# A graph kernel that fetches one edge tile in 22 row by row, and stores its results later

## The chip, the cores and the metric

The kernel runs on one core of one Trainium2 chip. The metric is the time of one execution on the device in microseconds (us). A core has several engines with instruction queues of their own, each working in order: TensorE (PE, matrix products; PEld is its loading of weights), VectorE (DVE), ScalarE (ACT), GpSimd (POOL) and SyncE (SP). SP, ACT and POOL also issue DMAs. Where a line of a profile says SPq or ACTq, it is an instruction that the engine's queue issues itself, such as a DMA.

## The reference

The input is a graph with 12,500 nodes of 256 features and 212,500 edges, sorted by destination. Each edge has a source, a destination and one of 8 types.

```python
h = jnp.maximum(_layernorm(x, axis=-1), 0.0)
hx = jnp.einsum('ni,rio->rno', h, weight)          # 8 weights of 256 x 256
msg = hx[edge_type, src]
agg = jax.ops.segment_sum(msg, dst, num_segments=12500)
out = x + agg * 0.5**0.5 + h_bias + (h @ loop_weight) * 0.5**0.5
```

## The kernel before

**Order of the sums.** The kernel does not compute 8 products per node and then gather them. It first adds up, for each destination and each type, the normalized rows `h` of the sources, and multiplies these sums by the weights afterwards. The edges stand in 1581 tiles of 128 places, two tiles to a unit. For each tile the 128 rows of `h` that its edges name are brought into a buffer `msg` (128 rows of 256 float32). PE multiplies them by a one-hot matrix of destination and type (`edge_sums`, line 1005, four matmuls a tile), so that a unit's sums per destination and type stand in PSUM (`ps`). DVE adds them to a ring of sums in SBUF (`acc`, line 1031). When all edges of a group of 128 nodes are through, PE multiplies the group's sums by the weights (`group_work`, line 1187, 36 matmuls a group), DVE adds `x` and the bias (lines 1200 and 1201), and once four groups are ready SP stores them with one DMA of 512 KB (line 1206). There are 98 groups; the last two are stored on their own (line 1203).

**Phases.** In the first 140 us or so the rows of `x` are normalized and written to `h32` in DRAM. The first 100 tiles gather rows of `x` itself and normalize them in place on ACT. All later tiles fetch from `h32`.

**Two ways to fetch a tile.** The usual one is an indirect DMA on POOL's queue (`gather`, line 915), one instruction for the 128 rows. The other is used for one tile in SINGLE = 28, those with `t % 28 == 27`, once `h32` has been complete for long enough and not for the last 16 tiles. Its 128 rows are fetched by 128 DMAs of 1 KB, 64 on SP's queue and 64 on ACT's (`load_sources`, line 939). Before each 32 rows the queue loads their addresses into registers with one TENSOR_LOAD (line 931). PE counts the 128 arrivals on one of four semaphores before it sums the tile.

**The written order.** The order of all instructions is written out by hand (`tc.manual_schedule`). A loop runs over the tiles; in step `t` it emits the sums of tile `t`, the gathers for tiles further ahead (64 ahead at first, 24 from about tile 370 on, down to 8 at the end: `goal`), and parts of the other work. A gather also waits for the latest unit summed at that point of the order. For a row-fetched tile the step FAR = 36 tiles ahead takes the buffer (`begin_fetch`); HOLD = 8 steps later its instructions begin to be emitted, FETCH = 4 per step on each queue:

```python
if t + FAR >= gathered and single_rows(t + FAR):
    begin_fetch(t + FAR)
while gathered < min(NT, goal(t)):
    gather(gathered)
    gathered += 1
fetch(FETCH)
```

The message buffers are a pool of 33 pairs of tiles (MSGS = 66), taken in turn. The rows of `x`, of `h` for the nodes' own part, and the results share a pool of six buffers of 512 KB (`rowp`). The result is added into the buffer that held the group's `x`, and the store reads it from there.

**What else is in these queues.** SP also loads `x` and `h` for the next four groups (line 1137) and, once per block of 128 units, the indices of a later block (line 393). ACT loads that block's `spans` (line 405, eight small DMAs), and clears parts of the ring early on (line 1040). From 300 us on ACT computes nothing. An instruction that waits holds up all that follow in its queue: in SP's, a store that waits for its sums stands in front of the row fetches emitted after it.

## Time and profile before

| | |
|---|---|
| median of 3 runs | 1983.34 us (1980.15 to 1984.99) |
| the profiled execution | 1982.09 us; span 1980.4 us |
| mean granted TensorE clock | 0.949 |
| busy: PE, DVE, POOL, ACT | 1711.7, 1309.2, 1457.9, 159.2 us |
| indirect DMAs on POOL | 1431 from `h32`, 100 from `x` |
| row DMAs | 3200 on SP, 3200 on ACT |
| DMA over the span | 279.45 MB, mean 141 GB/s |

In the lines of the profile a group of instructions stands as line, engine, operation, result <- operands, count, followed by busy time, mean duration and the idle time in front of it with what ended it. In the views of one line, three numbers with strokes are the shortest, the median and the longest duration in ns, followed by the first and the last start in us. A wait line reads: who waited, for whom, total us, times, longest. A line of the timeline reads: start, duration, what, and in brackets the idle time before it.

### The profile page before, as it was taken

Reading aid. Unit: us, or ns where it says so; the run is one execution under the profiler, and the core shown is the slowest. Engines: PE = TensorE matmul, PEld = TensorE weight load, DVE = VectorE, ACT = ScalarE, POOL = GpSimd, SP = SyncE. Lnnn points to the kernel's source line nnn. Section 1 sums busy time; section 2 is a strip of 40 time slices with the busy share of each in tenths; the row PEclk is TensorE's granted clock in tenths of the full one; section 3 lists DMA queues with packets and bytes.
Section 4 is the critical chain, followed back from the end, with each engine's and each line's share of the span. In section 5 each row is a group of like instructions: output and inputs, shape, how many; then the busy total and the mean of one; then the engine's idle time right before and its main releaser. Section 6 shows DMA issues by size and latency. Waiting matters only on the chain. (4 is left out here: it accounts for less than half of the span.)

```text
span 1980.4 us, 41340 instructions
## 1 busy us (share of the span) xinstructions
PE 1711.7 (86%) x10161; PEld 1473.8 (74%) x10161; DVE 1309.2 (66%) x3272; ACT 159.2 (8%) x334; POOL 1457.9 (74%) x1557
## 2 busy tenths in 40 slices
PE   2348999998899888889998898888989989899998
PEld 1247898997777777778777777777777767687897
DVE  6769767886665677656678565578666567665653
ACT  6777200000000000000000000000000000000000
POOL 7677776677777777777777777777777777777774
PEclk8559999999999999999999999999999999999999
DMA  7993444443444444444434444444444344444432
GB/s 252 358 301 103 126 126 134 140 140 107 138 128 122 149 132 120 141 130 121 149 111 141 132 119 143 141 119 141 129 122 142 109 144 130 120 140 125 127 115 78
DMA packets 158363, 279.45 MB, mean 141 GB/s; under 512 B 35376, under 2 KB 109126, under 8 KB 158118
## 3 DMA queue, kind: packets, MB, share of 16 engines
q0 software_dynamic: 73488, 200.77, 34.5%
q1 hardware_dynamic: 76584, 72.73, 11.9%
q10 hardware_dynamic: 8046, 3.30, 0.9%
q8 instruction: 80, 1.31, 0.3%
q14 instruction: 165, 1.35, 0.2%
HBM read 251.06 MB, written 25.60 MB: 140 GB/s over the span
## 5 line engine op out<-in xcount | busy, mean ns | idle before, releaser
L915 POOL DMA_INDIRECT msg<-h,gidx x1431 | 1361.2, 951 | 458.6 <-issue 335.6
L1005 PEld LDWEIGHTS ps<-oh,msg 128*128 128x128 f32 x6324 | 942.1, 198 | 408.1 <-DMA msg<-h,gidx 258.7
L1005 PE MATMUL ps<-oh,msg 128*128 128x136 f32 (+2 forms) x6324 | 1022.8, 291 | 226.3 <-DMA msg<-h,gidx 139.0
L1187 PE MATMUL po<-w,acc 128*128 128x256 f32 x3136 | 891.0, 389 | 15.4 <-DVE acc L1031 15.3
L1031 DVE TENSOR_TENSOR acc<-acc,ps 128x352 f32 x791 | 408.8, 517 | 413.0 <-PE ps L1005 402.1
L1187 PEld LDWEIGHTS po<-w,acc 128*128 128x128 f32 x3136 | 519.0, 193 | 52.1 <-DVE acc L1031 18.6
L1069 DVE SCALAR_TENSOR_TENSOR acc<-types,pt 128x256 f32<-128x256 bf16 (+1 forms) x688 | 247.3, 411 | 67.6 <-PE pt L1051 61.9
L967 DVE TENSOR_TENSOR oh<-fixed,cols 128x544 f32<-128x544 f32 (+1 forms) x396 | 285.8, 722 | 0.0
L915 POOL DMA_INDIRECT msg<-in_x_dram,gidx x100 | 94.8, 948 | 41.4 <-issue 30.1
L1187 PE MATMUL po<-wl,self_t 128*128 128x256 f32 x392 | 115.5, 420 | 3.5 <-DVE acc L1031 1.8
L1187 PEld LDWEIGHTS po<-wl,self_t 128*128 128x128 f32 x392 | 73.8, 210 | 12.6 <-DVE acc L1031 3.1
L853 ACT ACTIVATE msg<-msg,shift,rstd 128x256 f32<-128x256 f32 x100 | 50.8, 586 | 4.4 <-DVE stats L817 3.6
L853 ACT ACTIVATE xt<-xt,shift,rstd 128x256 f32<-128x256 f32 x98 | 50.0, 587 | 7.0 <-DVE shift L850 6.1
L809 DVE BATCH_NORM_STATS2 stats<-xt 128x6 f32<-128x256 f32 x98 | 34.3, 412 | 23.5 <-DMA xt<-in_x_dram 22.7
L1200 DVE TENSOR_TENSOR xr<-xr,po 128x256 f32<-128x256 f32 x98 | 40.4, 412 | 13.4 <-PE po L1187 12.2
L1123 DVE CAST types<-pt 128x512 bf16<-128x512 f32 x22 | 15.2, 691 | 49.6 <-PE pt L1119 49.6
L1056 DVE COPY self_t<-pt 128x256 f32<-128x256 f32 x98 | 40.7, 415 | 8.5 <-PE pt L1051 5.4
L1051 PE MATMUL pt<-ident,hr 128*128 128x128 f32 x196 | 38.9, 281 | 7.2 <-DMA hr<-h 5.3
L442 DVE TENSOR_SCALAR moves<-fixed 128x271 int32<-128x271 int32 (+1 forms) x90 | 40.6, 452 | 4.4 <-DVE acc L1031 3.0
L1201 DVE TENSOR_TENSOR xr<-xr,po 128x256 f32<-128x256 f32 x98 | 41.2, 421 | 3.4
L444 DVE COPY_PREDICATED fixed<-moves,fixed 128x311 int32<-128x311 int32 (+14 forms) x90 | 38.0, 422 | 3.1
L1051 PEld LDWEIGHTS pt<-ident,hr 128*128 128x128 f32 x196 | 25.6, 153 | 10.6 <-DMA hr<-h 5.6
(162 smaller groups left out, 349.1 us busy)
## 6 DMA issues: line engine op xcount, KB each, us to landing
msg<-h ACTq DMA_DIRECT2D x3200, 1.0 KB
msg<-h SPq DMA_DIRECT2D x3200, 1.0 KB
msg<-h,gidx POOLq DMA_INDIRECT x1431
xt<-in_x_dram SPq DMA_DIRECT2D x24, 512.0 KB
h<-xt SPq DMA_DIRECT2D x24, 512.0 KB
xr<-in_x_dram SPq DMA_DIRECT2D x24, 512.0 KB
hr<-h SPq DMA_DIRECT2D x24, 512.0 KB
out_dram<-xr SPq DMA_DIRECT2D x24, 512.0 KB
```

The costliest lines, as they stand in the source:

```text
L442: nc.vector.tensor_single_scalar(m, packed[:, :n], 1 << (bit + k), op=ALU.bitwise_and)
L853: nc.scalar.activation(row, row, AF.Relu, bias=shift[:n, j : j + 1], scale=rstd[:n, j : j + 1])
L915: i = nc.gpsimd.indirect_dma_start(out=msg[t], out_offset=None, in_=table[:, :], in_offset=bass.IndirectOffsetOnAxis(ap=gidx[b][:, at : at ...
L967: j = nc.vector.tensor_tensor(o[:, k : k + v, :i, :width], iota_f[:, :width].unsqueeze(1).unsqueeze(1).to_broadcast([P, v, i, width]), of. ...
L1005: j = nc.tensor.matmul(ps[:, c, first : first + width], m[:, c * P : (c + 1) * P], o[:, :width], start=(i == 0 and c == 0), stop=(end and ...
L1031: i = nc.vector.tensor_tensor(a, a, ps, op=ALU.add)
L1051: in_run("turns", nc.tensor.transpose(pst[:, c, :n], rows_[:n, c * P : (c + 1) * P], ident[:n, :n]), c == KC - 1)
L1056: nc.vector.tensor_copy(got["self", g][:, :, :n], pst[:, :, :n])
L1069: i = nc.vector.scalar_tensor_tensor(acc[:, :, r, s0 : s0 + n], of, float(r + 1), pst[:, :, :n], op0=ALU.is_equal, op1=ALU.mult)
L1187: i = nc.tensor.matmul(got["out", g][:n], lhs, rhs, start=(r == R and c == 0), stop=(r == R - 1 and c == KC - 1))
L1200: nc.vector.tensor_add(rows_[:n, k, :], rows_[:n, k, :], outs[g % 2][:n, 1, :])
L1201: nc.vector.tensor_add(rows_[:n, k, :], rows_[:n, k, :], got["out", g][:n])
```

## The change

Three constants and the place of the stores change. SINGLE goes from 28 to 22, so that one tile in 22 is fetched row by row. FAR goes from 36 to 44, so that such a tile's buffer is taken 44 tiles ahead of its sums. The store of four groups' results is no longer emitted when they are finished but STORE = 24 steps later; whatever is left is emitted after the loop. HOLD, FETCH and the pools stay. Everything behind the changed lines moves by one line (939 becomes 940), and by a few more towards the end.

```diff
-SINGLE = 28
+SINGLE = 22
 FETCH = 4
 SOURCES = 32
 BY_SP = (0, 2)
 HOLD = 8
-FAR = 36
+FAR = 44
+STORE = 24
...
                 elif k == XG - 1:
                     first = plan.starts[XG * q]
-                    nc.sync.dma_start(
-                        out[first : d0 + n].rearrange("(k p) d -> p k d", p=P), rows_)
+                    stores.append((done["tile"] + STORE, lambda: nc.sync.dma_start(
+                        out[first : d0 + n].rearrange("(k p) d -> p k d", p=P), rows_)))
...
                     gather(gathered)
                     gathered += 1
+                while stores and stores[0][0] <= t:
+                    stores.pop(0)[1]()
                 fetch(FETCH)
...
             while held():
                 advance(None)
+            while stores:
+                stores.pop(0)[1]()
             state["general"] = nc.values_load(flag[0:1, 0:1], min_val=0, max_val=1)
```

## The prediction

> **What bounds the kernel now.** First the page: span, busy shares and the costliest group.

> ```profile
> span 1980.4 us, 41340 instructions
> PE 1711.7 (86%) x10161; PEld 1473.8 (74%) x10161; DVE 1309.2 (66%) x3272; ACT 159.2 (8%) x334; POOL 1457.9 (74%) x1557
> L915 POOL DMA_INDIRECT msg<-h,gidx x1431 | 1361.2, 951 | 458.6 <-issue 335.6
> L915 POOL DMA_INDIRECT msg<-in_x_dram,gidx x100 | 94.8, 948 | 41.4 <-issue 30.1
> ```

> PE has the largest share (86%), POOL only 74%, but POOL's idle time belongs to "issue", a wait for nothing. So next the timeline of POOL in the middle, POOL's gathers of line 915 between 600 and 1950 us, and three stretches of the windows (columns PE, PEld, DVE, ACT, POOL).

> ```profile
> 1001.74 0.95 POOL L915 DMA_INDIRECT msg<-h,gidx  x1 [0.30 <-DMA msg<-h,gidx]
> 1002.99 0.95 POOL L915 DMA_INDIRECT msg<-h,gidx  x1 [0.30 <-issue]
> 1004.24 0.94 POOL L915 DMA_INDIRECT msg<-h,gidx  x1 [0.30 <-issue]
> ...
> L915 POOL DMA_INDIRECT msg<-h,gidx x1073: 942/946/1279, 600.2 to 1948.9; - x179
> ...
> 250.00:300.00 50.00, 50.00 (x334) 46.25 (x333) 31.32 (x66) 3.82 (x2) 35.69 (x39) 1.00 0.44 125
> 1000.00:1050.00 50.00, 43.79 (x253) 37.30 (x252) 35.11 (x79) 0.00 (x0) 37.79 (x41) 0.93 0.44 130
> 1850.00:1900.00 50.00, 49.80 (x295) 45.76 (x296) 29.63 (x62) 0.00 (x0) 37.80 (x40) 1.00 0.40 119
> ```

> A gather starts every 1.25 us, whatever the releaser column names: 0.95 busy and 0.30 between. From 600 to 1949 us there are 1072 such steps in 1348.7 us, 1.258 each. PE is full only early (250 to 300) and late (1850 to 1900); at 1000 us it has 6 us free in 50. The waits agree: PE waits for gathered messages, and SP for the sums in front of its stores.

> ```profile
> PE ps L1005 <- DMA msg<-h,gidx: 139.0, 218, 3.4
> PEld ps L1005 <- DMA msg<-h,gidx: 258.7, 372, 3.8
> SPq L1206 <- DVE acc L1031: 245.6, 16, 24.0
> SPq L1206 <- DVE xr L1201: 186.3, 5, 87.7
> ```

> No line there names a row-fetched tile: those arrive in time. So POOL, with 1531 gathers at 1.25 to 1.26 us, sets the pace.

> **Fewer gathers.** The row fetches are counted in the list of DMA issues and placed by line 939's rows.

> ```profile
> msg<-h ACTq DMA_DIRECT2D x3200, 1.0 KB
> msg<-h SPq DMA_DIRECT2D x3200, 1.0 KB
> ...
> L939 ACTq DMA_DIRECT2D msg<-h x3200: 217/228/835, 229.7 to 1843.9; - x189
> L939 SPq DMA_DIRECT2D msg<-h x3200: 227/228/1229, 232.4 to 1905.7; - x189
> ```

> Each of the two queues issues 64 rows per fetched tile: 50 tiles, t = 167, 195, ..., 1539. The same conditions with 22 in place of 28 give t = 175, 197, ..., 1561, which is 64 tiles. POOL loses 14 gathers: 14 x 1.258 = 17.6 us. If nothing else came late, the profiled 1982.1 us would become 1964.5.

> **More rows.** The two queues gain 14 x 64 = 896 rows each, and have 22 tiles of time, not 28, for one fetched tile. In the old rhythm 27 gathers give 27 x 1.258 = 34.0 us; in the new one 21 give 26.4 us. What a fetched tile costs its queue is read where a queue runs without a gap: from one TENSOR_LOAD (line 931, addresses of 32 rows) to the next is half a tile.

> ```profile
> L931 ACTq TENSOR_LOAD <-single x9: 2239/2280/2332, 227.0 to 331.4; - x9
> ...
> L931 ACTq TENSOR_LOAD <-single x11: 2248/2279/2355, 403.3 to 535.8; - x11
> ...
> L931 ACTq TENSOR_LOAD <-single x11: 2249/2307/2513, 1590.9 to 1722.3; - x11
> ...
> L931 SPq TENSOR_LOAD <-single x4: 2057/2158/2212, 427.9 to 466.7; - x4
> ...
> 920.57 5.01 ACTq L405 DMA_DIRECT2D spans<-in_dst_dram  x8
> ...
> L405 ACTq DMA_DIRECT2D spans<-in_dst_dram x35: 317/434/1652, 359.0 to 1590.5; - x35
> ...
> L1206 SPq DMA_DIRECT2D out_dram<-xr x24: 384/415/426, 227.9 to 1950.9; - x24
> L1137 SPq DMA_DIRECT2D xr<-in_x_dram x25: 371/405/2164, 129.3 to 1906.0; - x25
> L1137 SPq DMA_DIRECT2D hr<-h x25: 459/512/2182, 130.0 to 1819.5; - x25
> ```

> ACT: 104.4 us for 8 halves, 132.5 for 10, 131.4 for 10; together 368.3 / 28 = 13.15, so **26.3 us a tile** (26.1 to 26.5 by stretch). SP: 38.8 us for 3 halves, one load of x among them: 12.8 to 12.9, or 25.7 a tile; the 24 stores and some 45 loads of x and h at 0.4 to 0.5 us, spread over 64 tiles, add 0.5: 26.2 to 26.3. ACT adds its 35 loads of spans at up to 5.01 / 8 = 0.63: about 20 us in all. POOL needs 26.4 us for the same 22 tiles. The three are level, and that is the heart of this prediction: the row queues have had a quarter of their time free, and after the change they have none.

> ACT's sum, the slower of the two: its first TENSOR_LOAD at 227.0 stays, since the clear that stands in front of it waits for PE (row below); 128 halves x 13.15 = 1683; spans 20; the last row is issued at about 1930. Its landing shows nowhere by itself: the nearest row is a gather's landing, 2.79 us, in the chain that ended last; I bound it by 1 and 3 and take 2.5. Tile 1561 can be summed at 1933.

> ```profile
> 227.04 1.91 ACT L1040 ACTIVATE acc<-zero 128x2048 f32<-128x2048 f32 x1 [16.06 <-PE po L1187]
> ...
> 1955.17 2.79 DMA msg<-h,gidx
> ...
> L1005 PE MATMUL ps<-oh,msg x80: 312/313/417, 1936.7 to 1967.5; 128*128 128x176 f32 x80
> ...
> 1955.36 2.23 PE L1005 MATMUL ps<-oh,msg 128*128 128x176 f32 x12 [1.38 <-DMA msg<-h,gidx]
> 1958.00 0.86 PE L1005 MATMUL ps<-oh,msg 128*128 128x176 f32 x4 [0.41 <-DMA msg<-h,gidx]
> ```

> A tile has four matmuls of line 1005, so the last 80 are tiles 1561 to 1580, and 1561 starts at 1936.7 now. From there to 1982.1 are 45.4 us; some 2 of them are waits for gathers that would have landed. 1933 + 43.4 = 1976.4 for an execution like the profiled one. With gathers alone tile 1561 would start at 1919. The rows, 14 us late by then, give back 12 of the 17.6 us.

> **Lead of 44 tiles and later stores.** The longer lead holds a buffer 8 tiles longer. Of 66 tiles' buffers, 24 tiles of gathers ahead plus two or three fetched pairs are in use; I cost it at nothing, bounded by 0 and one gather step per fetched tile if a gather had to wait for a buffer. The stores' 432 us of waiting on SP (245.6 + 186.3) disappear from in front of the rows: SP will reach a store after its data is ready. That saves no time by itself, because PE never waited for a fetched tile; it is what lets SP take the extra rows at all. What stands behind a store in SP's queue (rows, loads of x and h, the indices of a later block) is pulled earlier by it. The result buffer is held 24 tiles longer of some 65 tiles per four groups, and its next user is two rounds off: nothing. The last stores stay where they are, at the end of the program. What is new: SP and ACT, without slack, run just in time, so that loads of x, h and indices come some 20 tiles after their place in the program. The first use of x or h is 30 tiles or more after it, that of the indices about 20: a wait of 0 to 4 us on DVE, five times, which DVE (66% busy) mostly hides.

> [...]

> **Rivals.**

> *The rows hide (chance 0.25).* A fetched tile at or below 26.1 us, as in ACT's first stretch, less waiting between POOL's and ACT's delays: the whole 17.6 us are gained, 1964.5. For it: the bound is missed by only 1 or 2%. Against it: the other two stretches.

> *The row queues are slower when they never rest (0.20; slower than before).* Each 0.1 us on a fetched tile costs 63 x 0.1 = 6.3 us at the end, and from 26.5 us on the time passes 1989. The rows of line 931 over the whole run show where this would come from:

> ```profile
> L931 ACTq TENSOR_LOAD <-single x100: 2216/2300/3672, 227.0 to 1831.0; - x100
> L931 SPq TENSOR_LOAD <-single x100: 2044/2180/3600, 228.9 to 1893.3; - x100
> ```

> If one TENSOR_LOAD in eight took the longest 3.67 us, a tile would cost 0.34 more: 1976 + 21 = 1997. Against it: in 227 to 331 us both queues were full, and ACT's halves were the shortest of all.

> *Both queues take turns at a shared generator (0.02).* Rows of 0.228 us would queue behind the other's 0.228: 64 x 0.456 + 5.6 = 34.8 us a tile, 540 us more. Against it: the stretch from 227 to 331 with both busy and no such lengthening. [...]

> *PE takes over (0.03).* It is full in 1850 to 1900, so the gain of the gathers after 1850 (1 of the 14) could go: 1966.

> **How the numbers follow.** The likeliest case (0.50) is the row queues as the new bound, 1970 to 1988, at 1976.4; the profiled execution (1982.1) lies 1.2 under the median of the runs (1983.3), so 1977 for the median. About 0.3%, 6 us, is what can be told from no change: below 1977.4 is faster, above 1989.3 slower. Faster: hidden rows 0.25, PE 0.03 and somewhat under half of the likeliest case, 0.20: 0.48. Slower: 0.22 by the two slow cases. The rest, 0.30, is within. The range runs from 1963 (hidden rows, with 1 us of spread) to 1996 (one long load in eight).

> **What would show it.** Right: 4096 rows per queue, 1517 gathers; SP's wait for stores near nothing; TENSOR_LOADs of ACT at a steady 13.1 to 13.2 us to the end, the last rows at 1920 to 1940; PE waiting before fetched tiles from about t = 500 on, and POOL ahead by more tiles. Wrong: ACT's last row well before 1915 (the rows hide), halves of 13.3 us or more (slower), or POOL's gathers waiting for buffers.

## The result, and the profile after

The kernel after takes **2155.1 us** (median of 4 runs, 2151.1 to 2158.5) against 1984.1 for the kernel before (a fourth run has joined the three of the table above): ratio 1.086, 95% interval 1.083 to 1.089. The forecast was 1977, and its range ended at 1996. The profiled execution has a span of 2149.4 us. When the first eight runs of the experiments were made, the kernel before itself took 2398 to 2401 us instead of 1980 to 1984, with pauses of some 0.7 us between and in instructions of SP and ACT, so those eight are compared only with each other, and the later ones with 1980 to 1984.

The page of after, and its queues:

```profile
span 2149.4 us, 45059 instructions
PE 1776.7 (83%) x10161; PEld 1514.3 (70%) x10161; DVE 1313.6 (61%) x3272; ACT 159.2 (7%) x334; POOL 1441.4 (67%) x1543
q1 hardware_dynamic: 78376, 73.65, 11.3%
q10 hardware_dynamic: 9838, 4.22, 1.2%
L916 POOL DMA_INDIRECT msg<-h,gidx x1417 | 1344.7, 949 | 644.1 <-issue 303.5
```

The counts came out as forecast: 14 gathers fewer (1417 and 100), and POOL busy for 16.5 us less. But POOL's idle time in front of the gathers rose from 458.6 to 644.1 us. The same stretches of the windows show the pace:

```profile
250.00:300.00 50.00, 50.00 (x334) 46.24 (x334) 31.23 (x66) 1.91 (x1) 35.50 (x38) 1.00 0.48 136
1000.00:1050.00 50.00, 39.45 (x219) 30.95 (x218) 21.71 (x47) 0.00 (x0) 32.26 (x35) 0.97 0.42 116
1850.00:1900.00 50.00, 42.38 (x248) 33.58 (x246) 26.07 (x59) 0.00 (x0) 33.77 (x37) 1.00 0.40 110
```

At 1000 us PE does 219 matmuls where it did 253, and POOL 35 gathers where it did 41. Every engine does less in the same time, so somebody waits for a transfer. The waits say for which:

```profile
PE ps L1006 <- DMA msg<-h,gidx: 211.0, 263, 3.2
PEld ps L1006 <- DMA msg<-h,gidx: 352.3, 415, 3.6
PE ps L1006 <- PEq L1003: 30.5, 9, 5.8
POOL msg L916 <- DMA msg<-h,gidx: 223.3, 291, 3.0
SPq L1207 <- DVE xr L1202: 51.1, 2, 50.8
SPq L1207 <- DVE acc L1032: 20.8, 8, 5.7
```

`msg<-h,gidx` is a gather. PE waits for **gathers** 211 us (139 before), for fetched tiles (the wait of line 1003) only 30 us, nine times. POOL itself waits 223 us for earlier gathers to land (54.9 before). In these sums each wait holds the 0.30 us that stand in front of every gather (303 ns at the least, in all 1530 steps of before and all 1516 of after); without them, 291 waits are 136 us in after, 145 are 11 us before.

Of the 169 us by which the span grew, 72 are PE's longer waits for gathers, 30 its waits for fetched tiles, and 65 are PE's own busy time: the same 10161 matmuls took 1776.7 us instead of 1711.7, at a mean granted clock of 0.921 instead of 0.949. A slower PE does not explain the loss, since PE waits longer for its gathers as well.

The row queues hardly rest either (SP waits for 71 us in all between 600 and 1800 us). In that time 82 steps of ACT from one TENSOR_LOAD to the next, half of its share of a tile, are 14.55 us on the mean, and 81 of SP's 14.62:

```profile
L932 ACTq TENSOR_LOAD <-single x83: 2223/2296/3352, 604.6 to 1797.8; - x83
L932 SPq TENSOR_LOAD <-single x82: 2114/2184/3498, 603.1 to 1787.4; - x82
```

A stretch of POOL's timeline:

```profile
953.51 0.94 POOL L916 DMA_INDIRECT msg<-h,gidx  x1 [0.30 <-issue]
955.29 0.94 POOL L916 DMA_INDIRECT msg<-h,gidx  x1 [0.83 <-PE ps L1006]
957.94 0.95 POOL L916 DMA_INDIRECT msg<-h,gidx  x1 [1.71 <-DMA msg<-h,gidx]
960.27 0.94 POOL L916 DMA_INDIRECT msg<-h,gidx  x1 [1.38 <-DMA msg<-h,gidx]
```

Before, a gather started every 1.25 us whatever the releaser column said. Here it starts after 1.78, 2.65 and 2.33 us: POOL has up to eight gathers in flight and then starts the next when the oldest has landed (when a gather of after starts, at most seven others are under way, in 563 of 1517 cases just seven, and none starts sooner than 0.257 us after the eighth before it has landed; 0.259 us in before, 0.26 in the run micro below). The chip has fewer gathers to do and is later with each.

**Why they land late** is in the trace's DMA packets. The trace gives a packet's queue but not its engine. These are the packets of after that follow each other without a gap in one stretch; others of POOL's queue, which overlap them, are left out (start in ns by the trace's own clock, 10,468 ns ahead of the views', queue, duration in ns, bytes; 1 is SP's queue, 10 ACT's, 0 POOL's; a 4-byte packet of 1 or 10 that follows a row is the write that counts it as done: with 896 rows more on queue 10, after has 896 packets of 1 KB and 896 of 4 bytes more there than before):

```
956570  10   46  1024
956613  10    9     4
956619  10   54  1024
956665  10   14     4
956673  10  102  1024
956769  10   12     4
956775  10  205  1024
956974  10   12     4
956980   1  180  1024
957154   1   12     4
957160  10  180  1024
957334  10   12     4
957340   1   47  1024
957383   1    9     4
957389   0  493  4096
957879   1  181  1024
```

Each packet begins within 10 ns of the end of the one ahead of it, whichever queue it is from: **all rows go through one DMA engine**, where a gather also has its share, by an even division two packets of 4 KB (a gather is 32 of those, and 16 counts of 4 bytes: 48,544 and 24,272 for the 1517 gathers of after; the page has 16 engines). Between 700 and 1500 us 1066 rows of ACT's queue lie clear of SP's loads and stores; 12 of them overlap another row by more than 10 ns. Of the gathers' packets that fit into the chain of rows, 23% take over 0.6 us; of those that overlap a row, and so are on another engine, 0.06% do, and 98 of 100 take 0.16 to 0.42 us. I call a gather's packet of over 0.6 us a slow one and count them per gather from 600 to 1600 us: **0.23 before, 0.56 after**. A gather has landed when the last of its 16 counts has come: of the gathers that start from 600 to 1600 us and show all 16, 569 in after, the 15th count comes 2.8 us after the start (median) and the 16th 10.3 us; in before 2.8 and 4.4 us. In after one count of sixteen is late, as one engine of sixteen would make it.

The rows wait there as well. Taking ACT's n-th row packet for its n-th issue, from 600 to 1800 us a row's packet ends 7.0 us after its issue in after (median) and 1.5 us before. A line of rows stands in front of that engine.

### The profile page after: what moved, and what is told of

Same layout as the page of the kernel before. It is cut to its first block, busy times and chain, and to the rows that moved or that the text cites. A ratio compares the mean times of both kernels' runs of the same rounds, so it can differ in the third digit from the quotient of the medians.

```text
span 2149.4 us, 45059 instructions
## 1 busy us (share of the span) xinstructions
PE 1776.7 (83%) x10161; PEld 1514.3 (70%) x10161; DVE 1313.6 (61%) x3272; ACT 159.2 (7%) x334; POOL 1441.4 (67%) x1543
## 5 line engine op out<-in xcount | busy, mean ns | idle before, releaser
L916 POOL DMA_INDIRECT msg<-h,gidx x1417 | 1344.7, 949 | 644.1 <-issue 303.5
L1006 PEld LDWEIGHTS ps<-oh,msg 128*128 128x128 f32 x6324 | 966.0, 203 | 538.4 <-DMA msg<-h,gidx 352.3
L1006 PE MATMUL ps<-oh,msg 128*128 128x136 f32 (+2 forms) x6324 | 1056.6, 298 | 333.1 <-DMA msg<-h,gidx 211.0
L1188 PE MATMUL po<-w,acc 128*128 128x256 f32 x3136 | 908.3, 395 | 13.0 <-DVE acc L1032 13.0
L1188 PEld LDWEIGHTS po<-w,acc 128*128 128x128 f32 x3136 | 531.2, 198 | 49.4 <-DVE acc L1032 14.3
L1188 PE MATMUL po<-wl,self_t 128*128 128x256 f32 x392 | 124.2, 446 | 3.4 <-DVE acc L1032 1.8
L916 POOL DMA_INDIRECT msg<-in_x_dram,gidx x100 | 94.8, 948 | 41.5 <-issue 28.0
L1188 PEld LDWEIGHTS po<-wl,self_t 128*128 128x128 f32 x392 | 79.1, 224 | 13.5 <-DVE acc L1032 2.6
L1201 DVE TENSOR_TENSOR xr<-xr,po 128x256 f32<-128x256 f32 x98 | 40.5, 413 | 15.4 <-PE po L1188 14.2
L1052 PEld LDWEIGHTS pt<-ident,hr 128*128 128x128 f32 x196 | 26.5, 157 | 10.3 <-DMA hr<-h 5.3
```

The lines of the kernel that those rows point to most:

```text
L916: i = nc.gpsimd.indirect_dma_start(out=msg[t], out_offset=None, in_=table[:, :], in_offset=bass.IndirectOffsetOnAxis(ap=gidx[b][:, at : at ...
L1006: j = nc.tensor.matmul(ps[:, c, first : first + width], m[:, c * P : (c + 1) * P], o[:, :width], start=(i == 0 and c == 0), stop=(end and ...
L1052: in_run("turns", nc.tensor.transpose(pst[:, c, :n], rows_[:n, c * P : (c + 1) * P], ident[:n, :n]), c == KC - 1)
L1188: i = nc.tensor.matmul(got["out", g][:n], lhs, rhs, start=(r == R and c == 0), stop=(r == R - 1 and c == KC - 1))
L1201: nc.vector.tensor_add(rows_[:n, k, :], rows_[:n, k, :], outs[g % 2][:n, 1, :])
```

## Experiments

The theory before the runs: that engine is full, 0.8 us per gathered tile plus 0.1 us per row (worked out from the paces of before and after, 1.213 and 1.345 us per tile). The rivals: the row queues' issuing; the buffers taken 44 tiles ahead; the later stores.

**1. SINGLE back at 28; SINGLE 22 alone; SINGLE 25; rows of two runs.**

```diff
 s28, s25 (from after)          b22 (from before)
-SINGLE = 22                    -SINGLE = 28
+SINGLE = 28      (s25: 25)     +SINGLE = 22
 two_engines (from after)
-    msg[t][r0 + i : r0 + i + 1, :].bitcast(U8), h32_bytes[:, bass.ds(v, D * 4)])
+    msg[t][r0 + i : r0 + i + 1, :].bitcast(U8).rearrange("p (c b) -> p c b", c=KC)[:, ::-1],
+    h32_bytes[:, bass.ds(v, D * 4)].rearrange("p (c b) -> p c b", c=KC))
...              (the sums of a fetched tile read its two halves in the same order)
```

s28: 

> The kernel after with SINGLE back at 28 (50 fetched tiles); FAR 44 and the later stores stay. Theory (one DMA engine carries every row and its share of every gather, about 0.8 us per gathered tile and 0.1 us per row, both worked out from the two paces of 1.21 and 1.345 us per tile): at 28 that engine needs about 1.21 us per tile, as in the kernel before, so 1975 to 1990 us. If buffers taken 44 tiles ahead or the later stores cost the time, it stays at 2100 or more. If the row queues' issuing is the bound, 26.3 us per 28 tiles hide and it is again 1975 to 1990.

b22: 

> The kernel before with SINGLE 22 alone (64 fetched tiles); FAR stays 36 and the stores are issued at once. Theory of the one DMA engine: 2150 us or more, since the rows are the same, and up to some tens of us on top where SP waits for results to store while rows are due. If FAR or the later stores cost the time: about 1965 to 2000. If the row queues' issuing is the bound: 2000 to 2150, with long waits of PE before fetched tiles.

s25: 

> The kernel after with SINGLE 25 (56 fetched tiles). Theory of the one DMA engine: 0.8 + (128 x 0.1 - 0.8)/25 = 1.28 us per tile, so about 2060 us, midway between 28 and 22. If the row queues' issuing is the bound, 26.3 to 27 us per fetched tile hide behind 25 tiles of 1.21 (30 us), and it is faster than at 28, about 1970. If buffers or stores are at fault: 2100 or more.

two_engines: 

> The kernel after with each row's DMA made of two runs of 512 bytes rather than one of 1 KB (the two halves of a message change places in the buffer, and the sums of fetched tiles read them so). As many row DMAs, waits and buffers as in the kernel after. Theory of the one DMA engine: a row's two runs go to two engines, each carries half, so about 0.8 + (64 x 0.1 - 0.8)/22 = 1.06 us per tile on the fullest engine: the gathers are on time again, their waits for DMA fall to those of before, and the time is 1960 to 2000 if a row of two runs is issued as quickly as one of one run; if it is issued more slowly, PE waits before fetched tiles instead and the gathers still are on time. If the row queues' issuing, the buffers or the stores are at fault: 2150 or more, with the gathers as late as after.

Measured beside 2398: s28 2387 (ratio 0.995, 0.993 to 0.998), s25 2498 (1.046, 1.041 to 1.051; a row fetch knows one tile of a pair only, so with an odd SINGLE every second fetched tile gets its partner's rows, as many), b22 2649 (1.106, 1.102 to 1.110), two_engines 4115 (1.72). So here SINGLE 22 alone makes the loss, and it grows step by step. But not by late gathers. PE's waits of b22, then of two_engines:

```profile
PE ps L1005 <- PEq L1002: 459.3, 54, 15.8
```

```profile
PE ps L1008 <- PEq L1004: 1526.8, 61, 30.6
```

In these runs PE waits for **fetched tiles**: SP needs 18.4 us for half of its rows of a tile in b22 (14.6 in after). The runs of this batch speak for the row queues, and leave the theory untested. The packets of a row of two runs speak for two engines: for ACT's 4096 rows queue 10 has 18,030 packets, 8192 more than in after, so that each row has two of data and two counts where it had one and one (and many of the 512-byte packets start in pairs, less than 30 ns apart). But such a row takes twice as long to issue: ACT's quickest half is 25 us instead of 13. As a remedy it is out.

**2. No rows; narrow rows; SINGLE 24.**

```diff
 nofetch: SINGLE = 4096      s24: SINGLE = 24
 narrow (from after; VectorE clears the buffer first)
-    msg[t][r0 + i : r0 + i + 1, :].bitcast(U8), h32_bytes[:, bass.ds(v, D * 4)])
+    msg[t][r0 + i : r0 + i + 1, :].bitcast(U8)[:, :64], h32_bytes[:, bass.ds(v, 64)])
...
```

nofetch: 

> The kernel after with no tile fetched row by row (SINGLE 4096): all 1581 tiles are gathered, SP and ACT issue no rows. Theory (one DMA engine carries all rows and its share of every gather): without rows that engine has 0.8 us per tile to do, far under POOL's pace, so gathers never land late and POOL issues one in 1.25 us to the end: 50 gathers more than the kernel before at 1.25 us, so 2040 to 2050 us where the kernel before takes 1984. If the gathers themselves, without any row, were what the DMA engines cannot keep up with: 2150 or more. Where the kernel before takes 2398, as in the runs so far, and rows are what is slower there, this one takes 2050 all the same and is faster than it.

narrow: 

> The kernel after, with 64 of the 1024 bytes of each fetched row moved (left out: the other 960; VectorE clears the buffer first). As many row DMAs, registers, semaphores and buffers. Theory of the one DMA engine, with what its packets took after (87 ns for a row, some 12 for the write that follows it): about 70 of 100 ns per row go, so 0.8 + (128 x 0.03 - 0.8)/22 = 0.94 us per tile and the gathers are on time: 1955 to 2010. If the row queues' issuing, the buffers or the stores cost the time: 2150, as after. If it is the number of packets on that engine and not their bytes: also about 2150, with the gathers still late.

s28_b: 

> The kernel after with SINGLE 28, FAR 44 and the later stores. Where the kernel before takes 1984: by the theory of the one DMA engine 1970 to 1990; by the buffers or the stores 2100 or more. Where the kernel before takes 2398: 2387, as run before.

s24: 

> The kernel after with SINGLE 24 (about 58 fetched tiles). Theory of the one DMA engine: 0.8 + (12.8 - 0.8)/24 = 1.30 us per tile, so 2080 to 2100 where the kernel before takes 1984, and each step from 28 to 24 to 22 costs. If the row queues' issuing were the bound, with 26.3 to 27 us per fetched tile and 24 tiles of 1.21 (29 us) to hide it: 1965 to 1975.

Measured beside 2401: nofetch 2344 (0.976, 0.972 to 0.981), s28_b 2385 (0.994), s24 2561 (1.066), narrow 2653 (1.104, as b22). nofetch was expected at 2050 and takes 290 us more without any row, so the rows alone are not what is slower in these runs. narrow is no test here, since its row queues issue as much as ever.

**3. The disputed cost by itself; after once more; SINGLE 44.** The micro kernel is POOL with 60 gathers back to back per stage, SP and ACT beside it issuing 160 rows each.

micro: 

> Not the kernel but the disputed cost by itself: 60 gathers of 128 rows back to back on POOL, five times, with a barrier after each time (nothing of the reference is computed). Beside them SP and ACT issue nothing; 160 rows of 1 KB each, one DMA a row; 160 runs of 4 KB each, one DMA a run; the same bytes as that and more in four DMAs of whole tiles of 512 KB; 160 rows of 64 bytes each. Theory of the one DMA engine (what is issued as one run goes to one engine, the same one every time, and a gather is done when its last engine is): the runs of 4 KB (about 4 times 46 ns each, at three or four in 1.25 us, beside 0.45 us of the gather's own) fill that engine and the gathers slow down from 1.25 us to 1.4 or more and wait for the one 8 before, while the whole tiles, spread over 16 engines, and the 64-byte rows leave them near 1.25; the rows of 1 KB lie between, 1.25 to 1.4. Were it the load of all DMA engines together, whole tiles would slow the gathers at least as much as the runs of 4 KB, which move fewer bytes; were it the number of row DMAs, the 64-byte rows would slow them as much as those of 1 KB.

after_here: 

> The kernel after, run beside the kernel before on the chips on which that one takes 2398 us. There SP needs 18.4 us for half of its rows of a fetched tile (13.9 in the trace of after), so 36.8 us per 22 tiles is 1.67 us per tile and the row queues are the bound: 2620 to 2660, like the kernel before with SINGLE 22 alone (2649), with PE waiting before fetched tiles. If the buffers taken 44 tiles ahead or the later stores did anything of their own, it differs from 2649 by more than 1%.

s44: 

> The kernel after with SINGLE 44 (32 fetched tiles). With 0.8 + (12.8 - 0.8)/44 = 1.07 us per tile the one DMA engine is far from full, and 37 to 42 us of SP per 44 tiles are under 1 us per tile, so neither holds it: between none fetched (2343) and one in 28 (2386), 2340 to 2370. If each fetched tile costs by its count, 32 x (2386 - 2343)/50 = 28 us over none: 2371.

Measured beside 1982: after_here 2155.8 (1.088, 1.086 to 1.090); s44 1983.5 (1.001, 1.000 to 1.002), where POOL's 91 waits for gathers are 27.8 us, none over 0.3, so no gather is late. In micro a gather's mean step over a stage was 1.25 us alone, 1.33 beside 1 KB rows, 1.25 beside runs of 4 KB, 1.25 beside four whole tiles of 512 KB, and **1.47 beside 64-byte rows**. POOL's timeline in that last stage:

```profile
363.98 0.94 POOL L35 DMA_INDIRECT msg<-in_x_dram,idx  x1 [1.23 <-DMA msg<-in_x_dram,idx]
366.18 0.95 POOL L35 DMA_INDIRECT msg<-in_x_dram,idx  x1 [1.25 <-DMA msg<-in_x_dram,idx]
368.56 0.94 POOL L35 DMA_INDIRECT msg<-in_x_dram,idx  x1 [1.43 <-DMA msg<-in_x_dram,idx]
```

While those rows ran, the gathers' long packets, those on the rows' engine, took 0.5 to 1.4 us each, and some 7 to 12 rows of 11 ns came between the two of one gather and those of the next. So the first theory falls in its second half: one engine, yes (whole tiles of 512 KB do no harm); filled by the rows' bytes, no (four times the bytes make no gather late, a sixteenth does more). What makes the gathers late is the **number of small rows** on that engine: beside them the gather's packets there take longer. By what means is not shown.

**4. Bytes against count in the kernel; FAR and the stores apart.** micro2 measures more sizes.

```diff
 wide2 (from after)
+TIMES = 2
-MSGS = 66            -AHEAD = 64
+MSGS = 60            +AHEAD = 58
...              (a row more behind h32, so that the last row has a next one)
+            wide[t] = wides.tile([P, TIMES * D], F32, name="wide")     # of 3 buffers
+            msg[t] = wide[t][:, :D]
-    msg[t][r0 + i : r0 + i + 1, :].bitcast(U8), h32_bytes[:, bass.ds(v, D * 4)])
+    wide[t][r0 + i : r0 + i + 1, :].bitcast(U8), h32_bytes[:, bass.ds(v, TIMES * D * 4)])
```

s28_c: 

> The kernel after with SINGLE 28, FAR 44 and the later stores. Where the kernel before takes 1982: if SINGLE alone makes the 171 us, 1975 to 1990; if buffers taken 44 tiles ahead or the later stores make it or part of it, 2020 to 2150. Where the kernel before takes 2398: 2387.

narrow_b: 

> The kernel after with 64 of the 1024 bytes of each fetched row moved (left out: the other 960), on a chip on which after takes 2155. If the bytes of the rows fill the one engine: 1955 to 2010. If it is the number of small rows there, as the gathers alone showed (1.47 us a gather beside 64-byte rows, 1.33 beside 1 KB rows, at about 6 rows per us): 2155 or more, up to 2300. Where the kernel before takes 2398: 2653, as run before.

wide2: 

> The kernel after with 2 KB fetched for every row, its own 1 KB and the next row's (not used), into three buffers of their own; 60 message buffers instead of 66 make room for them. The number of row DMAs stays. If the bytes of the rows on the one engine make the gathers late: some 40 ns more per row, 128 x 0.04/22 = 0.23 us per tile, so 2400 or more. If small rows are what stretches the gathers' packets there, and longer ones do it less, as 4 KB runs did beside gathers alone: below 2155, 1970 to 2100. If bytes do not matter in this range: 2140 to 2170.

micro2: 

> Not the kernel: 60 gathers of 128 rows on POOL, seven times. Beside them nothing; 160 rows on each of SP and ACT of 1 KB; of 2 KB; of 512 bytes; of 1 KB as two runs of 512 bytes; 1 KB on SP alone; 1 KB as sixteen runs of 64 bytes (nothing of the reference is computed). By the small rows: the gathers' mean step is 1.25 alone, 1.33 beside 1 KB as before, less beside 2 KB (1.25 to 1.30), more beside 512 bytes (1.35 to 1.45), 1.25 to 1.27 with one queue alone at half the rate. Two runs load two engines with rows of 512 bytes: if they are issued as fast as one run, 1.35 to 1.45; if at half the rate, below 1.30. By the bytes: 2 KB worst, 512 bytes better than 1 KB. [...]

micro2's windows of POOL, 45 us of each stage with rows under way (busy, gathers in brackets): alone; 1 KB; 2 KB; 512 bytes; two runs of 512; SP alone; sixteen runs of 64.

```profile
10.00:55.00 45.00, 34.05 (x36) 1.00 0.37 105
85.00:130.00 45.00, 31.75 (x34) 1.00 0.39 104
165.00:210.00 45.00, 34.01 (x36) 1.00 0.41 114
243.00:288.00 45.00, 29.99 (x33) 1.00 0.38 95
335.00:380.00 45.00, 34.04 (x36) 1.00 0.38 107
458.00:503.00 45.00, 34.02 (x37) 1.00 0.37 108
540.00:585.00 45.00, 34.02 (x36) 1.00 0.43 109
```

Only the stages of 1 KB and of 512 bytes from both queues, about 6 rows per us, lose gathers; mean steps over the stages 1.34 and 1.44, with 0.6 and 0.8 slow packets per gather in these windows against none in the others. Rows of 2 KB, issued as fast (6.6 per us), make no gather late; there only the rows themselves wait, up to 19 us from issue to the end of the packet. One queue alone (3.4 rows per us) does no harm. Rows of two runs are issued every 0.77 to 0.80 us per queue, of sixteen every 0.65, of one every 0.32.

narrow_b takes 2111.8 (1.066, 1.064 to 1.068), wide2 2117.9 (1.069, 1.068 to 1.071). The waits of narrow_b, then those of wide2:

```profile
PE ps L1007 <- DMA msg<-h,gidx: 204.8, 291, 5.2
POOL msg L917 <- DMA msg<-h,gidx: 158.2, 222, 3.0
PE ps L1007 <- PEq L1004: 16.5, 4, 5.8
```

```profile
PE ps L1012 <- PEq L1009: 276.0, 52, 12.2
POOL msg L922 <- DMA msg<-h,gidx: 41.9, 125, 1.8
L938 ACTq TENSOR_LOAD <-single x84: 2227/2296/3049, 610.1 to 1792.7; - x84
L938 SPq TENSOR_LOAD <-single x83: 2096/2182/3590, 599.4 to 1790.4; - x83
```

With a sixteenth of the bytes the gathers still land late (1.02 slow packets per gather), and 43 us come back. With twice the bytes they land **on time** (0.10 slow packets, POOL's wait below that of before), as micro2 said, and yet only 37 us come back, because now PE waits before the fetched tiles, 52 times. POOL is held back by PE there (218 us), so it is micro2 that shows the same at POOL's full pace. (wide2 has 65 of them: with 58 tiles ahead, tile 153 is one too.) The two rows of line 938 show how the fetched tiles come: 83 halves in 1182.6 us are 14.25 us on ACT, 82 in 1191.0 are 14.52 on SP, and SP waits some 20 us in all in that time, 1.2 of them for stores. A fetched tile takes its queues 28.5 to 29.0 us. That is a second bound, right behind the first: with 28.75 in place of 26.3, the prediction's own sum is 227 + 64 x 28.75 + 2.5 + 43.4 = 2113.

Whether this is the price of issuing is open. A row's packet ends 6.8 us after its issue in wide2 and 5.8 in narrow_b (medians, counted as for after), so the line in front of the engine is there in all three slow kernels, and it may slow the queues and make the fetched tiles late.

s28_c takes 2001.2 (1.010, 1.008 to 1.012): what is beside SINGLE costs some 20 us.

**5. The stores alone; no rows; one queue alone.**

```diff
 store28: SINGLE = 28, FAR = 36     nofetch_b: SINGLE = 4096     act44: SINGLE = 44, BY_SP = ()
```

store28: 

> The kernel before with the later stores alone (the kernel after with SINGLE 28 and FAR 36). If the later stores are what costs the 20 us between before and SINGLE 28 with both (they no longer hold SP, so that SP and ACT issue rows at the same time more often): 1995 to 2005. If it is FAR 44: 1975 to 1985.

nofetch_b: 

> The kernel after with no tile fetched row by row, where the kernel before takes 1982. All 1581 gathers at 1.25 us: 50 more than before, so by the pace of POOL 2040; from SINGLE 44, which takes 1983.5 with 32 fetched tiles, 32 x 1.25 more: 2023. If PE sets the pace as much as POOL, less: 1990 to 2010.

act44: 

> The kernel after with SINGLE 44 and all rows on ACT's queue (BY_SP empty). 52.6 us of ACT for a fetched tile fit into 44 tiles of 1.22 (53.7), barely. If two queues at once make the gathers late, the 28 us for which POOL waits for them with SINGLE 44 and both queues go: 1955 to 1980. If not, or if ACT does not keep up: 1983 to 2010.

store28 1991.2 (1.005, 1.003 to 1.006): the stores make half of the 20 us, FAR, by what is left, the other half; neither expectation held whole. nofetch_b 2029.1 (1.024, 1.022 to 1.026), between its first two expectations. act44 2007.0 (1.013, 1.011 to 1.015): PE waits for ACT. The 28 us that its expectation hoped to win were not there, since no gather of s44 is late. With one queue a row's packet ends 0.9 us after its issue, and ACT's steps of 32 rows are 13.44 us on the mean, 26.9 us for 64 rows.

```profile
PE ps L1006 <- PEq L1003: 211.8, 29, 22.6
L916 POOL DMA_INDIRECT msg<-h,gidx x1449 | 1375.8, 949 | 464.1 <-issue 372.6 <-PE ps L1006 63.6 <-DMA msg<-h,gidx 11.6
L932 ACTq TENSOR_LOAD <-single x89: 2193/2277/3732, 605.4 to 1788.4; - x89
```

The runs beside 1980 to 1984, together:

| kernel | us | fetched tiles | slow packets per gather | POOL waits for gathers, us | of that over 0.30 each | PE waits for fetched tiles, us |
|---|---|---|---|---|---|---|
| nofetch_b | 2029 | 0 | 0.05 | 9.4 | 0 | 0 |
| s44 | 1983.5 | 32 | 0.28 | 27.8 | 0 | 0 |
| act44 | 2007 | 32 | 0.11 | 11.6 | 0 | 211.8 |
| before | 1981 | 50 | 0.23 | 54.9 | 11 | 0 |
| store28 | 1991 | 50 | 0.38 | 57.6 | 15 | 0 |
| s28_c | 2001 | 50 | 0.47 | 67.5 | 17 | 0 |
| after | 2155 | 64 | 0.56 | 223.3 | 136 | 30.5 |
| narrow_b | 2112 | 64 | 1.02 | 158.2 | 92 | 16.5 |
| wide2 | 2118 | 65 | 0.10 | 41.9 | 4 | 276.0 |

The count of slow packets ranks these kernels only roughly: narrow_b has the most and is faster than after.

With FAR 44 and the later stores, the first 32 fetched tiles are worth 45.6 us (nofetch_b to s44), 1.4 each, a gather step and a little; the next 18 cost 18 us together (to s28_c); the next 14 cost 154 (to after). No version here beats the kernel before.

## Why the prediction was wrong, point by point

- **POOL sets the pace, 14 gathers fewer are worth 17.6 us**: right as far as it goes. By nofetch_b and s44 a fetched tile is worth 1.4 us while the rows do no harm.
- **More rows: the step that failed first.** A row was priced on the queue that issues it and nowhere else. On the one engine that carries it, it delays gathers, and gathers were what the prediction itself called the pace. Nothing in the sum stood for that, so no rival did either. In after POOL's waits for late gathers grew from 11 to 136 us; wide2 shows that part alone gone, and 37 us come back.
- **26.3 us a tile on the row queues: mis-sized.** wide2, where they hardly rest, has 28.5 to 29.0, after 29.1 to 29.2. For one queue alone 26.3 is nearly right (26.9 in act44). The rival "slower when they never rest" had the mechanism and the threshold (26.5 us) but priced one long load in eight, 0.34 us a tile, 1997. With the measured 28.75 the sum gives 2113. My 26.3 came from stretches of 39 to 133 us picked because they had no gap; the mean over 1200 us holds what such stretches leave out. From row to row it is 0.35 us in after on the mean, 0.336 before, 0.334 in act44. The landing, taken as 2.5 us and bounded by 3, is mis-sized too: 7.0 us in after at the median.
- **The forecast sign**: with the late gathers away the late fetched tiles end the run at 2118 (wide2), with rows of 64 bytes the late gathers end it at 2112 and PE hardly waits for rows (narrow_b). Each was seen without the other at a loss of over 6%; in after they overlap and do not add up.
- **FAR at nothing, stores at nothing**: each costs about 10 us at SINGLE 28 (the stores by store28, FAR by what is left). The stores' waits did fall in after, from 432 to 72 us, as forecast; in s28_c they only fall to 342. With them the slow packets per gather rise from 0.23 to 0.38 and 0.47, with as many rows. That the rows of the two queues then fall together more often fits (counting a queue as issuing while its rows start less than 4 us apart, both do so in 685 of the 1200 us from 600 on in s28_c, in 623 before, in 1040 in after), and so does micro2's single queue, but it was not tried by itself.
- **The shared generator** and **PE takes over**: no run shows a generator that the two queues share, and nothing of that size is seen (from row to row 0.334 us with one queue in act44, 0.35 with two in after); of the second nothing is seen.
- **What the trace before had shown.** POOL already waited 54.9 us for gathers, 145 times. The prediction put those waits aside because the steps were 1.25 us whatever the releaser, and for most of them that was right: 0.30 us of each is the usual gap. But 11 us are more than that, one wait was 1.9 us, and 0.23 packets per gather were slow; without rows (nofetch_b) no wait is over 0.3 us and 0.05 are slow. That was the sign that some gathers already had no room left.
- Of the signs named ahead, the counts came true; ACT's halves were 14.55 us on the mean (over 13.3: "slower"), SP's waits for stores fell to 72 us, the last row was issued at 2070, not 1920 to 1940, and PE waited before gathers, not before fetched tiles.

Open: what inside the engine makes a gather's packet slow, and how much of the fetched tiles' 28.5 to 29.2 us is issuing and how much the line in front of the engine. A cost by the count of rows alone does not explain that 2 KB rows, at 6.6 per us, do no harm to the gathers. SINGLE 22 alone was run only beside 2398 us.

## What to carry to other kernels

Before work is moved from a few wide transfers to many small ones, see in the packets whether a single DMA engine carries them all (as the rows of after), add up its load, and ask which other transfers have a share of it: in after the last of a gather's 16 counts came 10.3 us after its start, the one before it 2.8. Price a queue that is to lose all its slack by its mean over the whole run, not by its best stretches. When a change stands on a resource with "room", look for the waits that already name it.

## What was not expected of the hardware

- Beside gathers, rows of 64 bytes (mean step 1.47 us) and 512 bytes (1.44) did more harm than rows of 1 KB (1.33), and 2 KB and 4 KB none (1.25), at about the same 6 rows per us. Beside rows of 2 KB only the rows wait, up to 19 us, and not the gathers.
- A transfer of two runs of 512 bytes took 0.77 to 0.80 us to issue, one of sixteen runs of 64 bytes 0.65, one of a single run 0.32.
- A row's packet ended 0.9 us after its issue (median) where one queue alone issued, 1.5 with two queues at one tile in 28, and 7.0 at one in 22.
